# Five large blocks and 30 slots of on-chip memory, the tail's tiles ordered anew, and a 32-column product at 128 columns

## The chip, the core and the metric

The kernel runs on one core of one Trainium2 chip. The metric is device time in microseconds, the median of several runs. One more run was recorded by the hardware profiler; the profile and all queries of the trace come from it.

## The reference, cut to what matters

The input x has 16 batches of 256 tokens with 512 channels, all fp32. The first layer is a transformer block with 16 heads of 32: self-attention, cross-attention on a context, and a GELU MLP of 2048. The second layer is a recurrent block with 32 heads of 16:

```python
xxx = xa + sx * maa_x                       # xa: layer norm, sx: shifted minus xa
t = tanh(xxx @ maa_w1).reshape(B, L, 5, 32) # a product with 160 columns
m = einsum('blfd,fdc->blfc', t, maa_w2)     # five mixes w, k, v, r, g
xw, xk, xv, xr, xg = (xa + sx * (maa_j + m_j) for j in "wkvrg")
w = exp(-exp(time_decay + tanh(xw @ decay_w1) @ decay_w2))
r, k, v, g = xr @ Wr.T, xk @ Wk.T, xv @ Wv.T, silu(xg @ Wg.T)
# per head, token by token: out = r (u k v^T + s);  s = k v^T + w s
x = x + groupnorm(out) * g @ Wo.T
x = x + sigmoid(xr2 @ fWr.T) * (square(relu(xk2 @ fWk.T)) @ fWv.T)
```

## The kernel before

**Phases.** The program is written as a list of operations in phases. A is self-attention and B cross-attention, each over all 16 batches. Then come two parts of eight batches each: C0 is the MLP of batches 0 to 7, D0 the mix of the same batches (the products w, k, v, r, g), then C1 and D1 for batches 8 to 15. I0 and I1 are the "intra" work of the recurrence within groups of 8 tokens (elementwise products and sums on VectorE and GpSimd); I0 runs beside C1, I1 beside the tail. E is the tail for all 16 batches: states across the groups, reads of the states, group norm, output projection, and the last channel mix. Between phases, values go through DRAM (x1, x2, x3, and s_k, s_v, s_w, s_r, s_g, s_rp, s_ks, s_y, s_tot).

**Order.** `Sched.run` turns the list into a fixed order for each engine. It keeps a model of time, and at each step takes the operation that can start first; among equals the one with the lower index, moved by the table PRIO. DMAs all go through the one SyncE queue (L461), and their issue waits there in order. An operation can be taken only when its tiles have a place.

**Places.** `Memory` holds `SLOTS` = 34 slots of 1024 fp32 per partition (4 KB) and `BLOCKS` = 4 blocks of 4096 fp32 (16 KB), together 200 KB per partition, and the 8 banks of PSUM. A tile of class "4" takes a slot, one of class "2" half a slot (halves of one slot have one data type), one of class "16" a whole block, one of class "b" a quarter of a block. The weight tiles "wb" are of class "b". `SIZES` gives each phase a quota per tag. Earlier phases reserve what they still need: a later phase gets a place only from what the earlier ones, intra included, have neither taken nor reserved (`why_not`). So the next phase's loads and weight splits start in what is left over.

**Weights.** In A, B, C and D a weight is split into a high and a low part (`weight`, L534 and L535 with a scale, L551 and L472 without). A staging tile "st" is loaded, split on ScalarE, VectorE or GpSimd, and freed when the products for a folded bias (L522, L529) have also read it. A, B and D use 16 quarters, C uses 16 quarters and 16 slots.

**Cross-attention.** B holds up to 4 tiles of x, 3 of xh (normalised x, and the context) and 5 of xT (transposed and split; a batch needs 4). `tr` transposes (L593) and splits them (L467, L603), `attention_proj` uses them, two groups ahead of the scores.

**The mix.** `tmix` makes the 160 columns: 128 with W1, and 32 with W1b (12 products of 128 x 32 weights per batch). Tanh, and a split into `th`, high and low, follow. The parts go to a DRAM relay `tdr` and come back with other partitions, as S5 for the first four mixes and S5b for the fifth (high, low, and two rows of ones). `blend` multiplies them with W2 (L1045).

**The tail.** `tail_weights` loads eight quarters of weights (Wo, fr, fk, fv); `tail_tiles` makes the shift columns `sh0`, the constants of the channel mix, and clears two blocks VO and four slots RP (L1257), into which only the non-zero parts are written later. For each batch `states` loads VO from s_v in 8 pieces of 32 KB per half batch, multiplies (L1359), scans (L1366), reorders (L1367) and stores to `sdr`; `starts` loads it back and spreads it (L1291); `reads` transposes (L1397) and copies into RP (L1408); `heads` multiplies (L1426) and normalises; `output`, `residual` (L1471), `channels` and `finish` (L1471, L1512) do the rest. Once per four batches `states` calls `totals`, which loads s_tot, reorders (L1301), transposes (L1315) and copies it, and loads the start states s0. The intra's pieces are taken in between by `side`; I1 loads its tiles only after the gate of the last batch is stored to s_g.

Of the kernel before, what the change touches and what calls it, by code (L numbers as in the profile page):

```python
# [391 lines left out]
class Kern:  # L392
# [27 lines left out]
    def tile(self, tag, shape, name, dt=F32):  # L420
        n = 4 * int(np.prod(shape[1:]))
        h = H(tag, shape, dt, name)
        if n >= 512 or tag.startswith("p_"):
            h.phase, h.cls = self.nphase, "p" if tag.startswith("p_") else "16" if n > 4096 else tag[1] if tag in ("wb", "we") else "4" if n > 2048 else "2"
            self.mem.quota[h.phase, tag, h.cls] = self.sizes[tag]
        else:
            v = self.small.setdefault((tag, name, n), [0, []])
            if len(v[1]) < self.sizes[tag]:
                v[1].append(self.ktile(shape, name, dt))
            h = v[1][v[0] % self.sizes[tag]]  # L430
            v[0] += 1
# [466 lines left out]
class Rec(Kern):  # L898
# [7 lines left out]
    def mix_consts(self):  # L906
        I = self.I
# [3 lines left out]
        self.sh1 = self.shift_cols(1)  # L911

    def mix_weights(self):

        nc, I, tile = self.nc, self.I, self.tile
        W1, W1b, dw1 = tile("W1", [128, 4, 2, 128], "W1", F32R), tile("W1b", [128, 4, 2, 32], "W1b", F32R), tile("dw1", [128, 4, 2, 128], "dw1", F32R)
        for src, n, ws in ((I["L1_xattn_maa_w1"], 160, ((W1, 0, 128), (W1b, 128, 32))), (I["c_dw1"], 128, ((dw1, 0, 128),))):
            st = tile("st", [128, 4, n], "st")
            self.dma(st, lambda st=st: st(), lambda src=src: src.rearrange("(k p) n -> p k n", p=128), 2048 * n)
            for w, o, m in ws:  # L920
                self.split(4 * m, lambda st=st, o=o, m=m: st[:, :, o : o + m], lambda w=w: w[:, :, 0, :], lambda w=w: w[:, :, 1, :], [st], (w, 0), (w, 1))
# [20 lines left out]
        self.tdr, self.t2l = [], []  # L942
# [3 lines left out]
        for i in range(2):  # L946
            h = self.relay("tdr", [66, 5, 256], "tdr")
            self.dma(None, lambda h=h: h[64:66], lambda: fv(o2[64:66]).unsqueeze(1).to_broadcast([2, 5, 256]), 10240, r=[o2], w=[(h, 3)])
# [3 lines left out]
            self.t2l.append(h)  # L952

# [46 lines left out]
    def mix(self, src, rsrc, out, W, bs=range(B), side=None):  # L1000
# [15 lines left out]
        def tmix(b):  # L1016
# [4 lines left out]
            self.mm3((pt, 1), lambda: pt[0:32, 1, :], [lambda k=k: (W1b[:, k, 0, :], W1b[:, k, 1, :]) for k in range(4)], xs, 256, [W1b] + xx)  # L1021
            T, th = tile("T", [128, 2, 256], "tt"), tile("xj", [128, 2, 2, 256], "th", F32R)
            dr, S5, S5b = self.tdr[b % 2], tile("S5", [98, 4, 256], "S5", F32R), tile("S5b", [98, 256], "S5b", F32R)
            for i, p in ((0, 128), (1, 32)):
                emit("ACT", c_act(256), lambda i=i, p=p: nc.scalar.activation(out=T[0:p, i, :], in_=pt[0:p, i, :], func=AF.Tanh), [(pt, i)], [(T, i)])
                self.split(256, lambda i=i, p=p: T[0:p, i, :], lambda i=i, p=p: th[0:p, i, 1, :], lambda i=i, p=p: th[0:p, i, 0, :], [(T, i)], (th, (i, 1)), (th, (i, 0)))
            for x in range(2):
                self.dma(None, lambda x=x: dr[32 * x : 32 * x + 32, 0:4, :].rearrange("d j n -> j d n"), lambda x=x: fv(th[:, 0, x, :]), 131072, [(th, (0, x))], [(dr, x)])
            self.dma(None, lambda: dr[0:64, 4, :].rearrange("(x d) n -> d x n", x=2), lambda: fv(th[0:32, 1, :, :]), 65536, [(th, (1, 0)), (th, (1, 1))], [(dr, 2)])
            self.dma(None, lambda: fv(S5[0:32]), lambda: dr[32:64, 0:4, :], 131072, [(dr, 1)], [(S5, 0)])  # L1030
            self.dma(None, lambda: fv(S5[32:98]), lambda: dr[0:66, 0:4, :], 66 * 4096, [(dr, 0), (dr, 1), (dr, 3)], [(S5, 1)])
            self.dma(None, lambda: fv(S5b[0:32]), lambda: dr[32:64, 4, :], 32768, [(dr, 2)], [(S5b, 0)])
            self.dma(None, lambda: fv(S5b[32:98]), lambda: dr[0:66, 4, :], 66 * 1024, [(dr, 2), (dr, 3)], [(S5b, 1)])
# [200 lines left out]
class Tail(Rec):  # L1234
# [3 lines left out]
    def tail_weights(self):  # L1238
# [3 lines left out]
        W = {}  # L1242
        for n in ("Wo", "fr", "fk", "fv"):
            W[n] = [self.tile("wb", [128, 2, 512], "w_" + n) for _ in range(2)]
            for h, w in enumerate(W[n]):
                self.dma(w, lambda w=w: w(), lambda n=n, h=h: I["c_" + n][256 * h : 256 * h + 256, :].rearrange("(k p) c -> p k c", p=128), 524288)
        return W

    def tail_tiles(self):
        nc, I = self.nc, self.I  # L1250
        self.sh0 = self.shift_cols(0)
# [3 lines left out]
        self.RP, self.nrp = [self.tile("RP", [128, 2, 4, 4, 32], "RP") for _ in range(self.sizes["RP"])], 0  # L1255
        for t, n in [(t, 4) for t in self.VO] + [(t, 1) for t in self.RP]:
            self.emit(("POOL", "DVE"), (1250 * n, c_dve(1024 * n)), tuple(lambda t=t, e=e: e.memset(t(), 0.0) for e in (nc.gpsimd, nc.vector)), w=[t])  # L1257
# [45 lines left out]
    def totals(self, g):  # L1303

        nc = self.nc
        h = self.hin["tot"][0]
        t = self.tile("st", [128, 512], "tot")
# [9 lines left out]
        self.emit("PE", 432, fn, [t2, self.ident], [ps])  # L1317
        T = self.tile("tot", [128, 4, 4, 32], "tot")
# [9 lines left out]
        self.emit("DVE", c_dve(256), lambda: nc.vector.scalar_tensor_tensor(out=s0(), in0=m().unsqueeze(2).to_broadcast([128, 16, 16]), scalar=-1.0 / 16, in1=s0(), op0=ALU.mult, op1=ALU.add), [s0, m], [s0])  # L1328
        return T, s0

    def states(self, b):
        nc, tile, emit = self.nc, self.tile, self.emit
        if b % 4 == 0:
            self.tt = self.totals(b // 4)
# [201 lines left out]
SLOTS, BLOCKS = 34, 4  # L1536
SIZES = {
    "A": dict(wb=16, row=2, cf=1, sm=4, st=4, x=3, xh=1, xT=3, qk=3, V=3, T=6, E=9, PT=6, cT=5, mask=2, p_p=2, p_s=4, p_t=2, p_c=1),
    "B": dict(wb=16, row=2, cf=1, sm=4, st=4, x=4, xh=3, xT=5, qk=3, V=2, T=6, E=8, PT=6, cT=5, mask=4, p_p=2, p_s=4, p_t=2, p_c=1),
    "C": dict(wb=16, w=16, row=2, cf=1, sm=4, st=8, x=2, xh=2, xT=2, E=4, PT=1, cT=1, p_p=2, p_s=3, p_t=3),  # L1540
    "D": dict(wb=16, row=2, sm=4, st=4, x=1, xa=4, xx=2, W1=1, W1b=1, W2=5, dw1=1, dw2=2, t2l=2, T=3, xj=3, S5=2, S5b=2, s1=1, o=3, p_p=2, p_s=3, p_t=3, tdr=2),
# [106 lines left out]
```

## Time and profile before

| what | us |
|---|---|
| median of 3 runs (lowest, highest) | 3563.89 (3561.29, 3566.48) |
| the profiled execution | 3571.95 |
| its span | 3570.2 |
| PE (TensorE matmul) busy | 3273.7 |
| PEld (weight load, beside PE) busy | 2620.6 |
| DVE (VectorE) busy | 2843.3 |
| ACT (ScalarE) busy | 1882.5 |
| POOL (GpSimd) busy | 1395.8 |

Stages by PE's work in the trace: A to 718, B 734 to 1420, C0 1462 to 1800, D0 1800 to 2124, C1 2134 to 2490, D1 2490 to 2782, E 2782 to the end. The stretches between are where one stage hands over to the next.

To read the lines: L1359 is line 1359 of the kernel. "bank" is PSUM, "slot" and "block" the two kinds of on-chip places, "k_..." a constant; the tiles' own names are not in the trace, so a load of VO reads "block<-s_v". In a line of the timeline the first column is the start, the second the duration, in us; in brackets stands the idle time before it on its engine and what ended that. "SPq" is the SyncE queue that issues DMAs.

### The profile page before, as it was taken

The page shows a single profiled execution, that of the slowest core. Times are in us where ns is not written, and L with a number is a line of the kernel's source. Part 1 is how long each engine was busy: PE and PEld are TensorE (multiplying, and loading weights), DVE is VectorE, ACT ScalarE, POOL GpSimd, SP SyncE. Part 2 cuts the span into 40 slices and gives each one's busy share as a digit, 9 for nine tenths or more (in the row PEclk, how much of TensorE's full clock was granted, in tenths as well). Part 3 has the DMA queues.
Part 4 walks back from the last instruction along what each step waited for, and adds up shares of the span by engine and source line. Part 5 has one row for each costly group of instructions (what it writes and reads, how often), then busy time and mean ns, then how long its engine had stood idle before and what let it go on. Part 6 is the DMA issues. An engine that isn't in the chain of part 4 may idle for free. (4 is left out here: it accounts for less than half of the span.)

```text
span 3570.2 us, 72760 instructions
## 1 busy us (share of the span) xinstructions
PE 3273.7 (92%) x26978; PEld 2620.6 (73%) x26978; DVE 2843.3 (80%) x6696; ACT 1882.5 (53%) x4722; POOL 1395.8 (39%) x1853
## 2 busy tenths in 40 slices
PE   6999999989999999899999989999999558878899
PEld 4777877767777777788887879998787445555555
DVE  6888898868887788766788788899878688887653
ACT  4665666656666666433354454344444565554532
POOL 3444444444444444100021129994211476764110
PEclk9999999999999999899999999999999789998999
DMA  3111000021111110300134463343444877674420
GB/s 97 37 31 35 27 25 31 21 90 46 43 43 43 43 51 25 100 25 24 42 111 134 131 203 110 112 138 107 129 144 156 245 206 205 182 217 127 133 81 24
DMA packets 325051, 336.83 MB, mean 94 GB/s; under 512 B 40978, under 2 KB 228446, under 8 KB 324698
## 3 DMA queue, kind: packets, MB, share of 16 engines
q1 hardware_dynamic: 324698, 332.18, 30.5%
q8 instruction: 214, 3.51, 0.4%
q14 instruction: 139, 1.14, 0.1%
HBM read 199.92 MB, written 132.16 MB: 93 GB/s over the span
## 5 line engine op out<-in xcount | busy, mean ns | idle before, releaser
L721 POOL TENSOR_SCALAR slot<-slot,k_rin 128x256 f32<-128x256 f32 x1024 | 482.0, 488 | 691.8 <-DVE k_rin L718 624.8
L472 POOL TENSOR_TENSOR slot<-slot,slot 128x512 f32<-128x512 f32 (+9 forms) x394 | 540.4, 1393 | 312.7 <-ACT slot L551 133.2
L715 ACT ACTIVATE slot<-slot,k_nmx 128x256 f32<-128x256 f32 x1024 | 507.9, 498 | 199.3 <-DVE k_nmx L714 168.8
L486 PE MATMUL bank<-slot,block 128*128 128x256 f32 x1792 | 510.9, 285 | 0.2 <-ACT slot L467 0.2
L487 PE MATMUL bank<-slot,block 128*128 128x256 f32 x1792 | 508.0, 284 | 0.3 <-DVE slot L603 0.3
L488 PE MATMUL bank<-slot,block 128*128 128x256 f32 x1792 | 507.9, 283 | 0.0
L467 ACT ACTIVATE slot<-bank 128x512 f32<-128x512 f32 (+2 forms) x659 | 351.5, 565 | 270.4 <-PE bank L488 142.8
L486 PE MATMUL bank<-block,slot 128*128 128x512 f32 x1152 | 468.4, 407 | 11.3 <-ACT slot L557 10.2
L488 PE MATMUL bank<-block,slot 128*128 128x512 f32 x1152 | 453.8, 394 | 9.0 <-DVE slot L558 9.0
L487 PE MATMUL bank<-block,slot 128*128 128x512 f32 x1152 | 452.5, 393 | 0.0
L714 DVE CUSTOM_DVE_ANT_0 slot<-slot,slot 128x256 f32<-128x256 f32 x998 | 390.9, 436 | 0.0
L708 DVE SCALAR_TENSOR_TENSOR slot<-bank,slot 128x512 f32<-128x512 f32 x512 | 329.9, 680 | 44.3 <-PE bank L746 21.0
L1471 PE MATMUL bank<-block,slot 128*128 128x512 f32 x768 | 354.4, 613 | 1.6 <-DVE slot L1517 1.0
L486 PEld LDWEIGHTS bank<-slot,block 128*128 128x128 f32 x1792 | 344.1, 192 | 10.3 <-ACT slot L467 2.3
L487 PEld LDWEIGHTS bank<-slot,block 128*128 128x128 f32 x1792 | 344.0, 192 | 5.3 <-DVE slot L603 0.5
L488 PEld LDWEIGHTS bank<-slot,block 128*128 128x128 f32 x1792 | 344.1, 192 | 0.0
L487 PE MATMUL bank<-slot,slot 128*128 128x256 f32 (+2 forms) x960 | 309.1, 322 | 12.4 <-DVE slot L472 9.7
L486 PE MATMUL bank<-slot,slot 128*128 128x256 f32 (+2 forms) x960 | 307.9, 321 | 10.4 <-ACT slot L551 9.3
L734 PE MATMUL bank<-k_c,slot 128*128 128x128 f32 x2048 | 287.5, 281 | 25.1 <-POOL slot L721 10.9
L488 PE MATMUL bank<-slot,slot 128*128 128x256 f32 (+2 forms) x960 | 306.1, 319 | 1.5 <-DVE slot L558 1.5
L734 PEld LDWEIGHTS bank<-k_c,slot 128*128 128x128 f32 x2048 | 232.1, 143 | 96.3 <-POOL slot L721 64.1
L1471 PEld LDWEIGHTS bank<-block,slot 128*128 128x128 f32 x768 | 146.0, 196 | 168.6 <-issue 156.5
(195 smaller groups left out, 6639.3 us busy)
## 6 DMA issues: line engine op xcount, KB each, us to landing
slot<-in SPq DMA_DIRECT2D x153, 256.0 KB
slot<-x SPq DMA_DIRECT2D x64, 512.0 KB
x<-slot SPq DMA_DIRECT2D x48, 512.0 KB
slot<-in SPq DMA_DIRECT2D x32, 512.0 KB
sdr<-slot SPq DMA_DIRECT2D x128, 128.0 KB
slot<-sdr SPq DMA_DIRECT2D x32, 512.0 KB
s_k<-slot SPq DMA_DIRECT2D x16, 512.0 KB
s_w<-slot SPq DMA_DIRECT2D x16, 512.0 KB
```

What stands on the lines that cost most here:

```text
L467: self.emit(("ACT", "DVE"), (c_act(n), c_dve(n)), (lambda: nc.scalar.activation(out=out(), in_=in_(), func=AF.Copy), lambda: nc.vector.ten ...
L472: self.emit(("DVE", "POOL"), (c_dve(n), c_pool(n)), (lambda: nc.vector.tensor_tensor(out=out(), in0=in0(), in1=in1(), op=op), lambda: nc.g ...
L486: nc.tensor.matmul(o, lhsT=lh, rhs=rh, start=first and i == 0, stop=False)
L487: nc.tensor.matmul(o, lhsT=lh, rhs=rl, start=False, stop=False)
L488: nc.tensor.matmul(o, lhsT=ll, rhs=rh, start=False, stop=last and i == k - 1)
L708: emit("DVE", c_dve(512), lambda j=j, T=T: nc.vector.scalar_tensor_tensor(out=T(), in0=ps[j](), scalar=-scale, in1=mask(), op0=ALU.mult, o ...
L714: emit("DVE", c_dve(256) + 80, lambda T=T, j=j, qt=qt: nc.vector.tensor_tensor_reduce(out=T[:, qt, :], in0=T[:, qt, :], in1=negb[:, qt, :] ...
L715: emit("ACT", c_act(256, 1, 1), lambda T=T, Et=Et, j=j, qt=qt: nc.scalar.activation(out=Et[:, qt, :], in_=T[:, qt, :], func=AF.Exp, scale= ...
L721: emit("POOL", 470, lambda jj=jj, qt=qt: nc.gpsimd.tensor_scalar(out=E[jj][:, qt, :], in0=E[jj][:, qt, :], scalar1=rin[:, qt, jj : jj + 1] ...
L734: nc.tensor.transpose(pt[:, k, 128 * qt : 128 * qt + 128], E[j][:, qt, 128 * k : 128 * k + 128], self.ident())
L1471: self.nc.tensor.matmul(po(), lhsT=x[k // 2][:, k % 2, ts], rhs=w[k // 2][:, k % 2, :], start=k == 0, stop=k == 3)
```

## The change

Its core:

```diff
-            ... else tag[1] if tag in ("wb", "we") else ...
+            ... else tag[1] if tag in ("wb", "we", "rb") else ...
-SLOTS, BLOCKS = 34, 4
+SLOTS, BLOCKS = 30, 5
 SIZES = {
-    "B": dict(... x=4, xh=3, xT=5, ...
+    "B": dict(... x=3, xh=2, xT=4, ...
-    "C": dict(wb=16, w=16, ...
+    "C": dict(wb=20, w=12, ...
-    "D": dict(... s1=1, ...
+    "D": dict(... s1=2, ...
-    "E": dict(... RP=4, ...
+    "E": dict(... rb=4, ...
```

The total stays 200 KB per partition. C has 20 weights in blocks and 12 in slots. RP goes from slots into quarters of a block.

```diff
# mix_consts
-        self.sh1 = self.shift_cols(1)
+        self.sh1, self.sh0 = self.shift_cols(1), self.shift_cols(0)
# mix_weights: W1b [128, 4, 2, 32] becomes [128, 4, 2, 128], its 32 columns four times over
+                rows = lambda w, x, m=m: w[:, :, x, :].rearrange("p k (r c) -> p k r c", c=m)
+                self.split(512, lambda st=st, o=o, m=m: st[:, :, o : o + m].unsqueeze(2).to_broadcast([128, 4, 128 // m, m]), ...)
-            h = self.relay("tdr", [66, 5, 256], "tdr")
+            h = self.relay("tdr", [66, 4, 256], "tdr")
+            h = tile("S5b", [98, 256], f"S5b{i}", F32R)
# tmix
-            self.mm3((pt, 1), lambda: pt[0:32, 1, :], ...
+            self.mm3((pt, 1), lambda: pt[:, 1, :], ...
-            T, th = tile("T", [128, 2, 256], "tt"), tile("xj", [128, 2, 2, 256], "th", F32R)
+            T, th = tile("T", [128, 2, 256], "tt"), tile("s1", [128, 2, 256], "th", F32R)
-            for i, p in ((0, 128), (1, 32)):
+            for i, p in ((0, 128), (1, 96)):
                 emit("ACT", c_act(256), ... activation(out=T[0:p, i, :], in_=pt[0:p, i, :], func=AF.Tanh) ...
-                self.split(256, ... th[0:p, i, 1, :] ... th[0:p, i, 0, :] ...
+            self.split(256, lambda: T[:, 0, :], lambda: th[:, 1, :], lambda: th[:, 0, :], [(T, 0)], (th, 1), (th, 0))
-            self.dma(None, lambda: dr[0:64, 4, :]..., lambda: fv(th[0:32, 1, :, :]), 65536, ...)
-            self.dma(None, lambda: fv(S5b[0:32]), lambda: dr[32:64, 4, :], 32768, ...)
-            self.dma(None, lambda: fv(S5b[32:98]), lambda: dr[0:66, 4, :], 66 * 1024, ...)
+            emit(("ACT", "DVE"), ..., copy S5b[0:96] <- T[0:96, 1, :], [(T, 1)], [(S5b, 0), (S5b, 1)])
+            self.sub(256, lambda: S5b[32:64], lambda: T[32:64, 1, :], lambda: fv(S5b[32:64]), [(T, 1), (S5b, 0)], [(S5b, 1)])
```

Two S5b are kept for the whole phase, their rows 96 and 97 set to one at its start. The 32 columns come out four times, on all 128 partitions of PSUM, so that high, low and high part of the fifth mix are made where they are needed, without the way through DRAM.

```diff
+    def tail_consts(self):            # the column constants, taken out of tail_weights
     def tail_weights(self):
-                self.dma(w, ..., 524288)
+                self.dma(w, ..., 524288, [self.turn])
     def tail_tiles(self):
-        self.sh0 = self.shift_cols(0)
-        self.RP, self.nrp = [self.tile("RP", ...
+        self.RP, self.nrp = [self.tile("rb", ...
+        self.turn = H(None, None, None, "turn")
         for t, n in [(t, 4) for t in self.VO] + [(t, 1) for t in self.RP]:
-            self.emit(("POOL", "DVE"), ..., memset ..., w=[t])
+            self.emit(("POOL", "DVE"), ..., memset ..., [self.turn], [t, self.turn] if n > 1 else [t])
     def totals(self, g, within=None):
+        last = self.phase(within) if within else None
...
+        if last:
+            self.phase("E")
         T = self.tile("tot", [128, 4, 4, 32], "tot")
...
+        if last:
+            self.phase(last)
     def states(self, b):
-            self.tt = self.totals(b // 4)
+            self.tt = self.totals(b // 4) if b else self.first
# block_kernel
-        k.mix(rows(x3), lambda b: [(h3, b)], to, W, bs)
+        begun = []
+        def first_totals():
+            begun.append(1)
+            if n and len(begun) == 20:
+                k.hin = at
+                k.first = k.totals(0, k.now)
+        k.mix(rows(x3), lambda b: [(h3, b)], to, W, bs, first_totals)
     k.phase("E")
+    k.tail_consts()
+    k.tail_tiles()
     W = k.tail_weights()
-    k.tail_tiles()
```

`turn` is a handle without memory: each VO clear reads and writes it, RP's clears and the weights' loads read it. So the two VO clears come first, one behind the other, and RP and the weights behind both. The first totals are written into the list after the 20th of the second mix's 40 steps, with the PSUM bank and staging tiles of that phase, and with their result and the start states in tiles of E.

## Prediction

> **What bounds the kernel now.** I read the page's busy shares and slices first, then a table of busy time by stage, then PE's waits at each place where a stage hands over to the next. The page:
>
> ```profile
> span 3570.2 us, 72760 instructions
> PE 3273.7 (92%) x26978; PEld 2620.6 (73%) x26978; DVE 2843.3 (80%) x6696; ACT 1882.5 (53%) x4722; POOL 1395.8 (39%) x1853
> ```
>
> PE is busy 3273.7 of 3570.2 us. The change takes no product off PE, so what it can win lies in the 296.5 us in which PE idles. Stage by stage (columns: length; PE, PEld, DVE, ACT, POOL busy; granted clock; DMA share; GB/s):
>
> ```profile
> 718.00:734.00 16.00, 7.80 (x27) 4.23 (x26) 9.13 (x22) 7.58 (x12) 5.67 (x4) 0.88 0.85 287
> 734.00:1420.00 686.00, 660.35 (x5537) 536.72 (x5540) 555.36 (x1821) 446.27 (x1378) 288.30 (x543) 0.99 0.13 40
> 1420.00:1462.00 42.00, 24.32 (x230) 15.33 (x223) 32.14 (x69) 24.98 (x55) 15.35 (x19) 0.76 0.59 187
> ...
> 2124.00:2134.00 10.00, 0.40 (x4) 0.20 (x2) 8.19 (x15) 7.71 (x15) 3.79 (x3) 0.62 1.03 318
> ...
> 2782.00:2850.00 68.00, 28.59 (x924) 25.65 (x923) 41.21 (x77) 38.96 (x90) 33.06 (x32) 0.70 0.77 223
> 2850.00:3250.00 400.00, 322.48 (x4272) 205.47 (x4271) 353.60 (x608) 235.06 (x507) 280.21 (x244) 0.89 0.69 198
> 3250.00:3570.00 320.00, 290.58 (x2627) 175.42 (x2624) 181.60 (x404) 130.64 (x275) 42.71 (x78) 0.96 0.28 85
> ```
>
> The idle of PE is length minus its busy time: 8.2 us where attention A hands over to B, 17.7 from B to the first MLP, 9.6 from the first mix to the second MLP, 39.4 in the tail's first 68 us. From 2850 to 3250 VectorE is at 353.6/400 = 88% and carries the second intra beside the tail; from 3250 PE is at 91% and works off what has piled up. So a tail that starts earlier leaves a smaller pile, and the end comes earlier. The opening, in PE's order of time, and all that PE waits for in the tail:
>
> ```profile
> 2771.22 3.47 DVE L1257 MEMSET block<- 128x4096 f32 x1 [0.93 <-PE bank L488]
> 2775.86 3.52 POOL L1257 MEMSET block<- 128x4096 f32 x1 [20.89 <-PE bank L488]
> ```
>
> ```profile
> 2781.76 1.91 PE L1397 MATMUL bank<-k_c,slot 128*128 128x128 f32 x16
> 2786.07 1.90 PE L1359 MATMUL bank<-block,slot 128*32 128x128 f32 x64 [2.40 <-DMA block<-s_v]
> 2797.26 3.16 PE L1359 MATMUL bank<-block,slot 128*32 128x128 f32 x55 [9.29 <-DMA block<-s_v]
> ...
> 2802.72 3.27 PE L1359 MATMUL bank<-block,slot 128*32 128x128 f32 x64 [1.93 <-DMA block<-s_v]
> ...
> 2819.11 3.16 PE L1359 MATMUL bank<-block,slot 128*32 128x128 f32 x56 [13.11 <-DMA block<-s_v]
> ```
>
> ```profile
> PE bank L1359 <- DMA block<-s_v: 48.4, 8, 13.1
> ```
>
> Both VO blocks are cleared only at 2771 and 2776, when the second mix gives up the blocks of its weights; the tail's weights take the block before them (first issue at 2770). Four halves of the first two batches wait 2.4 + 9.3 + 1.9 + 13.1 = 26.7 us for VO's loads, of 48.4 in the whole tail. These loads share the DMA engines with 8 x 512 KB of tail weights.
>
> **The change, part by part.**
>
> *The tail's opening.* With five blocks the second mix uses four (16 weight quarters), so the first VO can be cleared and filled with batch 0 inside the mix, and the second takes the first block that is freed (the k weights' last product ends near 2763) instead of the third; the weights come behind both. The first half's product can then run before 2782, the second by 2782 instead of 2797: 15 us earlier. Batch 1 follows a refill later: its second half comes at about 2803 for 2819, 16 us. What cannot follow is the intra (its loads are issued at 2801 behind the last gate store, as now) and VectorE: it idles 68.0 - 41.2 = 26.8 us here, of which only that before the 88% stretch, in 2785 to 2830, can be filled, about 18. Bounds: no gain (VectorE's later work swallows it) to 18; below nothing by 5, since RP's four clears now wait for the VO clears (they ran at 2695 to 2729 now, POOL L1257, 0.95 us each; the first use is the copy at 2782). I take 12, near the upper rows, because two thirds of this idle is PE waiting for a load that the change moves.
>
> *Totals and shift columns.* The first totals are one 256 KB load, one copy (0.62), 4 transposes, one copy (0.68), all done by 2777 now, ahead of 2786. Moved, they gain nothing by themselves: 0. The wait they add: their PSUM bank, one of the mix's two p_p, is held until an E slot is free. Units of half slots: the mix keeps 52 of 60, the intra 15, so none is free for E before the mix winds down. The mix's other p_p users (front, tmix, decay) then queue for one bank for up to two batches of 36 us. Price 0 to 6; I take 1.
>
> *Fifth block at the other hand-overs.* A to B: the query weights can be split during A. Now the second half of their split is at 710.6 to 713.3, and the loads of the next weights are issued from 709; their staging tiles could be free when the bias products end, at 700. What then ends last is the load of the context:
>
> ```profile
> 710.61 2.73 DVE L535 SCALAR_TENSOR_TENSOR block<-slot,k_l2s,block 128x512 fp32r<-128x512 f32 x4
> ```
>
> ```profile
> 731.38 2.79 PE L593 MATMUL bank<-k_c,slot 128*128 128x128 f32 x12 [4.64 <-DMA slot<-in]
> ```
>
> One megabyte less in this stretch is 1.05 MB/287 GB/s = 3.7 us; at most all 8.2. I take 4, from -2 (fewer slots for B's early loads: A keeps 53 half slots, so 7 of 60 are free for them instead of 15 of 68). B to the first MLP: PE waits 17.3 us for staged weights, the longest one:
>
> ```profile
> 1457.47 0.66 PE L522 MATMUL bank<-slot,k_l3b 128*32 128x128 f32 x8 [10.02 <-DMA slot<-in]
> ```
>
> The same reasoning; B keeps 56 of 60 half slots, so 4 are free for staging instead of 6, so I take 4 of -3 to 10. First mix to second MLP: the 9.8 us wait is for the first GELU and the next weights; each pair gets its block one projection earlier (some 6 us), but staging slots are fewer: 2 of 0 to 6. First MLP to mix: PE is at 334.98/338, nothing to win.
>
> *Fewer x, xh and xT in B.* The fifth xT tile could be used ahead of the last projection. It isn't: the last projection's products end at 1023.9 and the four transposes follow at 1026.0, 1028.4, 1030.3 and 1031.9, the next projection at 1033.2, with scores, mixes and transposes of weights between. The cover is 9.3 us of other products per batch. Cost 0 to 2 per batch; I take 2 us in all for 15 batches.
>
> *Small product at full width.* 12 products per batch get a 128-column weight. Its loads, one narrow, one wide, in the first mix:
>
> ```profile
> L488 PEld LDWEIGHTS bank<-slot,slot 128*128 128x128 f32 x72 | 15.5, 215 | 0.9 <-DVE slot L558 0.4
> L488 PEld LDWEIGHTS bank<-slot,slot 128*32 128x32 f32 x28 | 3.8, 134 | 0.7
> ```
>
> That is +81 ns for each of 192 loads, 15.6 us if bare. But products of both widths start 0.12 us apart at full clock (narrow at 1915.06, 1915.18, 1915.29; wide at 1940.56, 1940.68, 1940.80), so the load lies beside the product before it: 0. In return three DMAs per batch (64, 32 and 66 KB) and their SP issues (3 x about 0.6 us) go, and the fifth tanh row set no longer passes DRAM; it is needed only four steps later, so 0. The splits into a four times wider W1b add about 0.5 us twice, at hand-overs: inside the range.
>
> The Trainium skill, "TensorE: Matmul & The Clock Gate", section "LDWEIGHTS (loading the stationary operand)", speaks against this edit: a load's time is its columns over 1.2 per ns, so 32 to 128 columns is 27 to 107 ns. By that rule 192 x 80 ns = 15.4 us would be added if nothing hid it, and the gain below would shrink to about 5 us. The row has a smaller ratio (134 to 215) and shows the start-to-start distance unchanged.
>
> **Sum.** Gains 12 + 4 + 4 + 2 = 22, costs 1 + 2 = 3, so 19 us, rounded to 20. The profiled execution took 3571.95 us (span 3570.2 and 1.75 around it): 3552. It lies 8.1 above the median of the three runs, 3563.89, so on their scale I forecast **3544**.
>
> **Rivals.**
> 1. *The opening is won and lost again.* If VectorE at 88% from 2850 to 3250 and the intra, whose start does not move, set the pace, the 12 us go and 4 + 4 + 2 - 3 = 7 remain: 3557. For: VectorE's and POOL's steps make up most of the chain of waits in this stretch. Against: PE idles 77.5 us there, and the last 320 us are PE's.
> 2. *Only the opening gains.* Staging slots, not blocks, limit the hand-overs; 12 - 3 = 9: 3555.
> 3. *Slower: the channel tiles of B.* With four xT tiles for four needed, all transposes must lie between the last projection of a batch and the first of the next. If the new order leaves this 6.6 us chain (1026.0 to 1032.6) partly bare, 2.5 us in each of 15 batches is 37 us: 3544 + 37 = 3581. It turns the sign from 20/15 = 1.3 us per batch, and is outside 0.2% from 1.8. For: no spare tile is left, and VectorE, which must split all four, is at 555/686 = 81%. Against: 9.3 us of cover.
> 4. *It doesn't do what it says.* The first VO gets no block early, because the mix's reservations or a block left partly filled keep it out: opening 0, hand-overs little: 3562.
>
> **How the numbers follow.** Chances: forecast 0.42, rivals one 0.13, two 0.12, three 0.25, four 0.08. A difference under 0.2% (7 us) is about what a measurement of this kernel can't tell from no change. Faster: the forecast, two, and most of one: 0.42 + 0.12 + 0.09 = 0.63; same: the rest of one and four: 0.12; slower: three: 0.25. Range: the best bounds (18 + 8 + 10 + 6, nothing lost) are 42 us, 3522, and the order being new throughout, 3518; the other end takes in rival three: 3582. The forecast's own range is 3525 to 3554.
>
> **What would show it.** Right: one VO clear during the second mix, the other near 2763 on today's clock, L1359's waits for s_v down from 48.4 by 20 or more, the four first halves 12 to 16 us earlier relative to the mix's last product; L535 into blocks before A's last group; narrow 128*32 loads gone with D's stage length unchanged at 324 and 292 us. Wrong: B longer than 686 us with waits at L593, or a second mix longer than 292 (bank held), or an opening that is shorter while 3250 to the end is no shorter.

## The result and the profile after

After takes **3591.54 us** (median of 4 runs, 3590.38 to 3596.53), before 3563.14 on the same chip: ratio **1.0077, 95% interval 1.0063 to 1.0092**. It is 28 us slower; 3544 was forecast, and the range ended at 3582. The profiled execution of after is 3590.38 us long, span 3588.6.

The page of after:

```profile
span 3588.6 us, 72653 instructions
PE 3289.7 (92%) x26978; PEld 2628.6 (73%) x26978; DVE 2875.0 (80%) x6693; ACT 1874.5 (52%) x4716; POOL 1415.7 (39%) x1866
```

PE's products are the same in number. VectorE executes 3 instructions fewer and is busy 31.7 us longer (2875.0 for 2843.3): the prediction has no term for this.

Stage by stage, read from the times at which SP issues the stores (first and last store of x1, x2, x3, the gate and the output), in the two profiled executions. The times were rounded before they were subtracted, so a row can be off by 1 us:

| from store to store | before | after |
|---|---|---|
| A's end to B's first | 78 | 64 |
| B | 653 | 650 |
| B's end to C0's first, C0 (7 batches) | 66, 283 | 64, 278 |
| to D0's first gate, D0 | 69, 250 | 79, 252 |
| to C1's first, C1 | 62, 325 | 58, **341** |
| to D1's first gate, D1 | 32, 251 | **38**, 251 |
| last gate to last output (the tail) | 778 | **790** |

Of C0 only seven batches are counted, since its eighth store comes behind D0's first gate.

These rows add up to +18 us; the rest of the 28 is that before's profiled execution lay 8 above its median and after's 1 below. So A to B, B, B to C0, C0 and D0 to C1 gave 14 + 3 + 2 + 5 + 4 us. The hand-over into the first mix, C1 beside the intra, the hand-over into the second mix, and the tail took 10 + 16 + 6 + 12, with 2 in D0.

The three windows of after that answer to those shown of before (hand-over A to B, and the tail's stretches, laid from 6 us later):

```profile
718.00:734.00 16.00, 14.55 (x97) 11.03 (x96) 10.06 (x19) 6.72 (x12) 6.89 (x4) 1.00 0.53 185
...
2856.00:3256.00 400.00, 311.81 (x4120) 195.85 (x4118) 353.56 (x554) 231.28 (x502) 262.21 (x226) 0.89 0.63 187
3256.00:3588.00 332.00, 306.55 (x2676) 183.66 (x2676) 197.91 (x426) 138.13 (x294) 67.71 (x102) 0.96 0.29 92
```

A to B, PE idles 1.5 us for 8.2. In the 400 us of the tail VectorE is as busy as before (353.6 us), but does 554 instructions for 608, and PE 311.8 us for 322.5: VectorE's instructions take longer on the mean.

The opening, VO's clears first, then PE's products on VO (timelines of after):

```profile
2476.29 3.52 POOL L1264 MEMSET block<- 128x4096 f32 x1
2767.37 3.52 POOL L1264 MEMSET block<- 128x4096 f32 x1 [6.05 <-PE bank L488]
```

```profile
2758.82 1.05 PE L1371 MATMUL bank<-block,slot 128*32 128x128 f32 x32
2760.24 1.05 PE L1371 MATMUL bank<-block,slot 128*32 128x128 f32 x32
...
2795.80 5.20 PE L1371 MATMUL bank<-block,slot 128*32 128x128 f32 x128 [7.95 <-DMA block<-s_v]
2813.11 3.39 PE L1371 MATMUL bank<-block,slot 128*32 128x128 f32 x64 [11.08 <-DMA block<-s_v]
```

```profile
PE bank L1371 <- DMA block<-s_v: 31.0, 4, 11.1
```

The first half product comes at 2759 for 2786, inside the mix. Against the last gate store (2789 before, 2795 after) the four halves are 33, 7, 10 and 12 us earlier, and the waits for s_v fall from 48.4 to 31.0. Still the first output comes only 4 us earlier against that store (178 us behind it for 182), and the last one 12 us later.

### The profile page after: what moved, and what is told of

Read it like the earlier page. It is cut to its first block, busy times and chain, and to the rows that moved or that the text cites. A ratio compares the mean times of both kernels' runs of the same rounds, so it can differ in the third digit from the quotient of the medians.

```text
span 3588.6 us, 72653 instructions
## 1 busy us (share of the span) xinstructions
PE 3289.7 (92%) x26978; PEld 2628.6 (73%) x26978; DVE 2875.0 (80%) x6693; ACT 1874.5 (52%) x4716; POOL 1415.7 (39%) x1866
## 5 line engine op out<-in xcount | busy, mean ns | idle before, releaser
L487 PE MATMUL bank<-slot,block 128*128 128x256 f32 x2048 | 581.9, 284 | 6.7 <-DVE slot L558 4.2
L486 PE MATMUL bank<-slot,block 128*128 128x256 f32 x2048 | 584.5, 285 | 0.8 <-ACT slot L467 0.5
L488 PE MATMUL bank<-slot,block 128*128 128x256 f32 x2048 | 581.5, 284 | 0.0
L487 PEld LDWEIGHTS bank<-slot,block 128*128 128x128 f32 x2048 | 394.1, 192 | 13.3 <-DVE slot L558 4.6
L486 PEld LDWEIGHTS bank<-slot,block 128*128 128x128 f32 x2048 | 394.0, 192 | 12.1 <-ACT slot L467 2.9
L488 PEld LDWEIGHTS bank<-slot,block 128*128 128x128 f32 x2048 | 394.0, 192 | 0.0
L1483 PEld LDWEIGHTS bank<-block,slot 128*128 128x128 f32 x768 | 149.4, 201 | 189.0 <-issue 166.6
L486 PEld LDWEIGHTS bank<-block,slot 128*128 128x128 f32 x1152 | 218.4, 190 | 65.2 <-issue 14.6
L488 PEld LDWEIGHTS bank<-block,slot 128*128 128x128 f32 x1152 | 217.4, 189 | 62.2 <-DVE slot L558 14.9
L486 PE MATMUL bank<-slot,slot 128*128 128x256 f32 (+1 forms) x704 | 237.5, 337 | 22.2 <-ACT slot L557 9.3
```

The lines of the kernel that those rows point to most:

```text
L486: nc.tensor.matmul(o, lhsT=lh, rhs=rh, start=first and i == 0, stop=False)
L487: nc.tensor.matmul(o, lhsT=lh, rhs=rl, start=False, stop=False)
L488: nc.tensor.matmul(o, lhsT=ll, rhs=rh, start=False, stop=last and i == k - 1)
L1483: self.nc.tensor.matmul(po(), lhsT=x[k // 2][:, k % 2, ts], rhs=w[k // 2][:, k % 2, :], start=k == 0, stop=k == 3)
```

## Where VectorE's time went

The groups that grew are the smallest instructions of the tail. `heads` makes the group norm's reciprocal root on VectorE in twelve steps of 64 elements per batch; here three of the steps, before and after (mean ns of one behind the comma):

```profile
L1442 DVE SCALAR_TENSOR_TENSOR k_gr<-k_gt,k_gr 128x64 f32<-128x64 f32 x48 | 15.2, 316 | 1.6
L1441 DVE TENSOR_TENSOR k_gt<-k_gt,k_gr 128x64 f32<-128x64 f32 x48 | 14.4, 299 | 1.6
L1440 DVE SCALAR_TENSOR_TENSOR k_gt<-k_gr,k_gv 128x64 f32<-128x64 f32 x48 | 13.3, 278 | 1.6
```

```profile
L1453 DVE TENSOR_TENSOR k_gt<-k_gt,k_gr 128x64 f32<-128x64 f32 x48 | 25.0, 521 | 1.6
L1452 DVE SCALAR_TENSOR_TENSOR k_gt<-k_gr,k_gv 128x64 f32<-128x64 f32 x48 | 21.5, 447 | 1.4
L1454 DVE SCALAR_TENSOR_TENSOR k_gr<-k_gt,k_gr 128x64 f32<-128x64 f32 x48 | 20.5, 426 | 1.6
```

All 192 steps take 64.9 us in before and 89.7 in after (the groups' means give 64.5 and 89.4); 192 times the shortest duration of each form is 40, so 25.0 and **50.0 us** are excess. The cause stands in the timelines of VectorE and GpSimd in after, side by side:

```profile
3016.06 0.30 DVE L1452 SCALAR_TENSOR_TENSOR k_gt<-k_gr,k_gv 128x64 f32<-128x64 f32 x1
3016.40 1.20 DVE L1453 TENSOR_TENSOR k_gt<-k_gt,k_gr 128x64 f32<-128x64 f32 x1
3017.64 1.19 DVE L1454 SCALAR_TENSOR_TENSOR k_gr<-k_gt,k_gr 128x64 f32<-128x64 f32 x1
...
3023.33 2.26 DVE L1453 TENSOR_TENSOR k_gt<-k_gt,k_gr 128x64 f32<-128x64 f32 x1
3025.62 2.26 DVE L1454 SCALAR_TENSOR_TENSOR k_gr<-k_gt,k_gr 128x64 f32<-128x64 f32 x1
```

```profile
3016.25 1.28 POOL L472 TENSOR_TENSOR slot<-slot 128x512 f32<-128x512 f32 x1
3017.48 5.05 POOL L472 TENSOR_TENSOR slot<-slot,slot 128x512 f32<-128x512 f32 x4
3022.49 0.72 POOL L472 TENSOR_TENSOR slot<-slot 128x256 f32<-128x256 f32 x1
3023.17 8.19 POOL L472 TENSOR_TENSOR slot<-slot,slot 128x1024 f32<-128x1024 f32 x4
```

The step at 3016.40 ends at 3017.60, 0.07 us behind the end of the product that GpSimd began at 3016.25 (3017.53). From there each step lasts as long as one product of the intra: 1.2 us beside products of 512 elements, 2.26 beside 1024, for 0.21 alone. It is so throughout: all 47 steps of after that take over 0.5 us, and all 23 of before, end 0.05 to 0.09 us behind the end of a GpSimd instruction, and none of those of up to 0.3 us lies inside one. In the model of time that makes the order, such instructions of the two engines never overlap (`port` in `Sched.run`); in the rows they do. The waits table shows none of it, since the wait lies inside the instruction: it is found by comparing a group's mean with its shortest.

The Trainium skill, "SBUF — State Buffer", section "SBUF: two separate sides", has the rule: VectorE (in some modes, or with two operands from SBUF) and GpSimd share a port pair, and whoever starts first keeps it for the whole instruction. The rows agree, at 2.3 us at the longest.

## Experiments

Chips differ (before took 3563 to 3572 us), so ratios are to before on the same chip. The bracket is the excess of the 192 small steps.

| | ratio (95%) | C1 | to D1 | tail | small steps, us |
|---|---|---|---|---|---|
| before | 1 | 325 | 32 | 778 | 64.9 (25.0) |
| after | 1.0077 (1.0063-1.0092) | 341 | 38 | 790 | 89.7 (50.0) |
| e1 after, steps as sums | 0.9978 (0.9969-0.9988) | 340 | 39 | 761 | 42.0 |
| e2 before, steps as sums | 0.9985 (0.9976-0.9995) | 328 | 32 | 771 | 42.1 |
| e3 memory alone | 1.0057 (1.0041-1.0073) | 337 | 39 | 796 | 65.0 (24.6) |
| e4 all but memory | 1.0014 (1.0005-1.0024) | 330 | 31 | 792 | 54.1 (13.3) |
| e5 after, bias on ScalarE | 1.0047 (1.0031-1.0064) | 334 | 38 | 792 | 90.7 (51.2) |
| e6 after, root in PSUM | 0.9962 (0.9947-0.9977) | 343 | 38 | 751 | 43 |
| e7 before, root in PSUM | 0.9992 (0.9981-1.0003) | 325 | 32 | 769 | 43 |
| e8 after, e5 and e6 | **0.9929 (0.9915-0.9944)** | 334 | 38 | 746 | 43 |
| e9 no early totals | 1.0045 (1.0029-1.0061) | 341 | 39 | 779 | 71.7 (31.7) |
| e10 no tail order | 1.0061 (1.0039-1.0082) | 344 | 41 | 781 | 73.7 (34.0) |
| e11 no wide product | 1.0005 (0.9993-1.0017) | 337 | 43 | 774 | 67.6 (27.6) |
| e12 memory and tail order | 1.0015 (1.0005-1.0025) | 337 | 43 | 779 | 72.3 (32.5) |
| e13 tail's blocks later | 1.0081 (1.0057-1.0104) | 340 | 42 | 786 | 95.5 (56.4) |
| e14 e8 and e13 | 0.9954 (0.9937-0.9971) | 334 | 37 | 754 | 43 |
| e15 normalise first | 1.0114 (1.0099-1.0129) | 342 | 40 | 790 | 88.0 (48.5) |
| e16 before, e5 and e6 | 1.0097 (1.0081-1.0112) | 340 | 35 | 795 | 43 |
| e17 normalise as sums | 1.0037 (1.0023-1.0051) | 334 | 38 | 788 | 89.0 (49.6) |
| e18 e8, normalise on ScalarE | 0.9946 (0.9929-0.9962) | 337 | 44 | 748 | 43 |

### The small steps, in the same order (e1, e2)

Each of the twelve steps becomes a sum over an axis of length one; the order stays, instruction by instruction:

```diff
-  nc.vector.tensor_tensor(out=t(), in0=t(), in1=r(), op=ALU.mult)
+  nc.vector.tensor_reduce(out=t(), in_=t().unsqueeze(2), axis=AX.X, op=ALU.add)
```

> The kernel after, in its own order, but the twelve small steps of 64 elements per batch with which the group norm makes its reciprocal root (L1446 to L1454) are replaced by sums over an axis of length one: same tiles, same sizes, same place in the order. The reciprocal root is left out by this, so the output is not the reference's. In the trace of after these 192 steps take 89.7 us, 50.0 more than 192 times their shortest durations, and each long one ends about 0.1 us behind the end of a GpSimd product; before they take 64.9, 25.0 more than their shortest. Sums (L1445) show no such lengthening. Port theory (the new order lays these steps beside GpSimd's products, VectorE paces the tail at 88%, and this is what the tail loses): the steps take about 45 us, VectorE loses some 45 us in the tail, and the time falls by 25 to 45 us, to 3547 to 3567. Rival (the steps are off the path, PE waits for other things): within 6 us of after, 3586 to 3598.

> The same replacement in the kernel before, again with its own order kept and the reciprocal root left out. Port theory: here only 25.0 us can go, so the time falls by 10 to 25 us, to 3538 to 3553, and the distance from after to before, 28 us, shrinks to 15 or less. Rival: within 6 us of before, 3557 to 3569, and the distance of 28 us stays.

The steps of e1, in the same places beside the same products:

```profile
L1454 DVE TENSOR_REDUCE k_gr<-k_gt 128x64 f32<-128x64 f32 x48 | 10.6, 220 | 1.6
L1453 DVE TENSOR_REDUCE k_gt<-k_gt 128x64 f32<-128x64 f32 x48 | 10.5, 220 | 1.6
```

No excess is left. After's time falls by 1.0077 - 0.9978 = 1.0%, some 35 us, and its tail by 29 us; before's by 0.15% (5 us; 10 to 25 were expected, a miss), its tail by 7. The two are then within 0.1% of each other: **the waits cost after 22 us more of tail than before**. In the 400 us from 2856 VectorE is then busy 332 us for 354, and PE 326 for 312 (e1's row):

```profile
2856.00:3256.00 400.00, 326.45 (x4306) 205.40 (x4304) 332.41 (x588) 244.60 (x540) 284.98 (x244) 0.90 0.67 195
```

Without the waits after's first output comes 14 us earlier behind the last gate store than before's (166, 181) and the last one 10 us earlier (761, 771). That fits a gain of the opening of the size forecast; it isn't shown to be the opening's alone, since the rest of the tail's order differs too.

### The small steps with one operand in PSUM (e6, e7)

One operand of each step lies in the PSUM bank that has just been read; the reference is computed in full:

```diff
-  r = tile("gs", [128, 64], "gr")
+  r = lambda: py().rearrange("p e a v -> p (e a v)")[:, 64:128]   # v, t stay in SBUF
```

> The kernel after, with one operand of each of the twelve small steps in PSUM, in the bank from which the last group's sum has just been read, so that no step has all its operands in SBUF; the whole reference is computed. The products L1429 (before) and L1441 (after), with one operand in PSUM, always take 0.68 us beside GpSimd. Port theory: no step over 0.5 us, 192 steps in 45 to 55 us against 89.7, the length from the last gate store to the end 760 to 772 for 790, and a total of 0.9965 to 1.0005 of before. Rival (the steps wait for GpSimd whatever they read, or the bank held some 4 us longer per batch stops PE): steps above 70 us or PE waits at L1438 for banks, and a tail of 780 or more.

> The same edit of the twelve steps in the kernel before. Port theory, with e2 as its size: 192 steps in 45 to 55 us against 64.9, the tail 768 to 776 for 778, total 0.997 to 1.000 of before; so that after with the edit (e6) ends within 0.2% of before with it, or below. Rival: tail 780 or more.

In e6:

```profile
L1454 DVE SCALAR_TENSOR_TENSOR k_gt<-bank,k_gv 128x64 f32<-128x64 f32 x48 | 10.7, 223 | 1.6
L1455 DVE TENSOR_TENSOR k_gt<-k_gt,bank 128x64 f32<-128x64 f32 x48 | 10.6, 220 | 1.6
```

No step takes over 0.23 us; the tail takes 751 us (760 to 772 expected) and the total is 0.9962, both better than the ranges given. The order behind these steps is a new one here, so the 10 us between e1 and e6 are not the steps'. Before gains 0.08%, not told from nothing, and its tail 9 us. With this hazard out of both, after is 0.3% (11 us) faster than before (e6, e7).

### The parts (e3, e4, e9 to e12)

Each kernel takes parts of the diff: the memory (SLOTS, BLOCKS, the sizes of B and C, RP in quarters), the tail's order (`turn`, tiles ahead of weights), the totals in the mix, and the wide product. For e3, for example:

```diff
-SLOTS, BLOCKS = 34, 4
+SLOTS, BLOCKS = 30, 5
```

> The kernel before with the memory part alone: five blocks and 30 slots, the sizes of B and C that go with them, RP in quarters of a block; the tail's order, the totals and the narrow product stay as before. If the memory part makes both the gains at the hand-overs and the losses: first store of B 14 us earlier than before, last store of the first layer's second half (C1) level with before, as after shows, and a total above before by 10 to 30 us. If the losses come from the tail's order, the totals or the wide product: the hand-over gains stay to the end, 3563 less some 15, 3540 to 3555. Port theory: whatever the part, the length from the last gate store to the end moves with the excess of the small steps, some 0.5 us per us.

> The kernel after without the memory part: four blocks and 34 slots and the sizes of before, RP in slots; the tail's order, the totals in the second mix and the wide product stay as in after. If the memory part makes the losses: no gain at the hand-over of A to B, C1 as before, total within 8 us of before, 3555 to 3571. If the other three parts make them: C1 or the tail longer by 15 to 30 us and a total of 3578 to 3600, above after's since the hand-over's 14 us are missing. Port theory: length of the tail against the excess of the small steps as in the other runs.

> The kernel after without the early totals: the first totals are made at the first states again, the rest as in after. So far the small steps wait for GpSimd 25.0 us in before, 50.0 in after, 24.6 with the memory alone, 13.3 with all but the memory. Theory of chance (no single part lays the steps beside GpSimd's products; every new order deals the meetings anew, between some 10 and 50 us): the excess is anywhere in 10 to 50, and the tail's length follows it by some 0.6 us per us around 764 (after: 790 at 50). Theory of one part (the totals' move does it): excess below 25 and tail below 778, and with the next two runs near 50.

> The kernel after without the tail's new order: weights ahead of the tail's tiles and no turn among the clears, with the memory, the totals and the wide product of after. Chance: excess of the small steps anywhere in 10 to 50. One part (the tail's order lays them there): excess 25 or less. Beside that, the opening: the half products of VO wait for s_v some 20 us longer and the first stores of the intra or of the output come 8 to 16 us later relative to the last gate than in after (178 us from there to the first output), as the prediction has it; if the opening is worth nothing, they come within 4 us.

> The kernel after without the wide product: 32 columns, the fifth mix through DRAM again. Prediction: the second mix's length (251 us from first to last gate store) within 3 us of after's, the cost of the wide loads being hidden. If the loads are not hidden: 6 to 8 us shorter than after's per mix. Chance: excess of the small steps anywhere in 10 to 50; one part (the wide product): 25 or less.

> The kernel before with the memory part and the tail's order alone; totals and product as before. Second MLP as in after and e3, 336 to 342 us. The opening's gain needs these two parts only: the distance from the last gate store to the first output is 170 to 180 (before 182, memory alone 189, after 178). Chance: excess anywhere in 10 to 50, total between 0.998 and 1.007 of before, 0.6 us per us of excess. If totals or wide product do harm of their own, total below 1.002 with an excess like after's.

No one part lays the steps beside the products: without the totals, the tail's order or the wide product the excess falls from 50 to 28 to 34 us, and without the memory part to 13. With all four parts it is no matter of luck from run to run: after, e5, e13, e15 and e17 have 48 to 56. Where memory and tail order are in, the tail goes with the excess: 761 us at 2 (e1), 774 at 28, 779 at 32, 790 at 50, or 0.6 us per us (e13, 786 at 56, lies below). It is no law: with no excess, e6, e8, e14 and e18 have tails of 746 to 754, and e3 and e4 lie above that line. In e4 VO is cleared only at 2769 and 2774, since no block is free for it before, and RP and the weights wait behind it: PE does 31 us of work in the opening's 85 us, for 46 of 86 in before. In e3 PE waits 17.7 us once for the spread start states (L1426).

The memory part alone makes the gain from A to B (64 us in e3, 77 in e4), 6 of the 9 to 10 us more into D0 (75 in e3, 71 in e4, 79 in after), the longer way into D1 (39 for 32), and most of C1 (337 for 325). The way into D0 also takes 76 us in e16, with four blocks and another order, so five blocks aren't needed for that.

With the tail's order left out (e10), the first store of s_y by the intra comes 15 us later against the last gate (102 for 87 us) and the first output 6 (184 for 178). But PE's waits for s_v are shorter there, 20.4 us for 31.0, where 20 more were expected. And s_y is as late in e9 (104) and e12 (106), which have the tail's order without the early totals, while before has 86 without either. So what the tail's order is worth by itself is not shown. The totals' held bank costs nothing that shows (D1 takes 246 to 252 us in the kernels without it, 243 to 253 in those with it). Without the wide product D0 and D1 take 253 and 245 us for 252 and 251, between the two ranges expected; D1 is as short in e10 and e13 (246, 245), which have it, so no cost of it shows.

### The second MLP (e5, e13, e15, e17)

```diff
# e5: L852
-  emit(("ACT", "DVE"), (c_act(256, 1), c_dve(256, 1)), (lambda ...activation, lambda ...tensor_scalar), ...)
+  emit("ACT", c_act(256, 1), lambda ...activation, ...)
# e13: the clears in tail_tiles
-  [self.turn], ...
+  [self.turn, (self.hin["g"][0], 8)], ...
# e15: PRIO
-  "C.lnst": 100, "C.lnrs": 400
+  "C.lnst": -400, "C.lnrs": -400
# e17: L575, L577, L580 on VectorE in C
+  nc.vector.tensor_reduce(out=xh[:, t, :], in_=x[:, t, :].unsqueeze(2), ...)
```

> The kernel after, with the MLP's bias adds (L852) given to ScalarE alone, as one of the two engines that could take them; nothing else is changed, and the order is made anew from there. From the first to the last store of x3 in the second MLP after takes 341 us, before 325, and memory alone (e3) 337; PE's waits there are for VectorE (L580, L558, L603), which has 58 bias adds of 0.49 us in after, 57 in e3 and 43 before, while ScalarE idles 60%. Theory (VectorE paces the second MLP, and the new places pushed bias adds onto it): 28 us of VectorE's work go from this stage, its length falls to 323 to 332 and the hand-over to the second mix from 38 to 32 to 36; the total falls by 8 to 20 us if the tail's small steps wait as in after (50 us), and more if fewer of them do. Rival (loads or splits are late since there are fewer free slots): the stage stays at 338 to 344.

> The kernel after, but both VO clears (and so RP's and the tail's weights behind them) also wait for the first gate of the second mix to be stored. In after the fifth block comes free at the end of the second MLP, and the tail takes it at once: 8 loads of s_v stand in SP's queue at 2481 to 2496, between the loads of the second mix's weights. Theory (the tail's early block disturbs the hand-over): from the last store of x3 to the first gate 32 to 34 us instead of 38, and PE's wait of 5.2 us at L486 before 2510 shorter; the opening of the tail (178 us to the first output) stays within 4 us, since 250 us of the mix are left to fill the block. Total 4 to 8 us below after, if the small steps still wait some 50 us. Rival (the hand-over is late because the second MLP's last GELU is): 37 to 40 us as before, and the total within 4 us of after's.

> The kernel after with the statistics of the MLP's layer norm taken first among equals (two priorities of the order changed, from 100 and 400 to -400). In after PE waits 6.0 us in the second MLP for the normalised x (L580), each gap of 1 to 2.4 us, and one such gap comes with a granted clock of 0.91 for its 20 us. Theory (the normalise chain, behind GpSimd's products, is what lengthens the second MLP): waits at L593 under 2 us and 332 to 337 us from first to last x3 for 341. Rival (VectorE as a whole is late there, whichever step is taken first): the waits move to L558 and L603, and the stage stays at 338 to 344.

> The kernel after, in its own order, but in the two MLP stages VectorE's three steps of the layer norm (L575, L577, and L580 where VectorE has it) are replaced by sums over an axis of length one, of the same size and place, that still wait for GpSimd's power step (L576). The normalisation is left out by this, so the output is not the reference's. In after, in front of PE's gaps of 1.30 and 1.08 us at 2333 to 2335, L577 takes 1.24 us and two L580 2.98 us (0.2 and 0.5 each elsewhere), between products of GpSimd. Port theory for the second MLP: no such step is lengthened, PE's waits at L593 go from 6.0 us below 3, and with them the granted clock's dips; the stage goes from 341 to 333 to 337 us, the total falls by 4 to 10 us. Rival (the order lays statistics, GpSimd's power step and the normalise too late in any case): the waits stay at 4 us or more and the stage at 338 to 344.

In e5 C1 is 7 us shorter, 334, outside both ranges (323 to 332, 338 to 344). Its order is new there, the bias adds between these stores are 47 in after and 37 before, and VectorE is busy only 3 us more in C1 of after than of before (299 for 296), so that VectorE's load is a part of the 16 us is not shown. In e13 the hand-over takes 42 us, longer than either side expected: the tail's loads in SP's queue are not what delays it. In e15 C1 stays at 342, as the rival had it, but the waits didn't move away from L593; they rose to 9.5 us. So taking the statistics first doesn't help.

Lengthened steps show here too. PE's waits in C1 for the normalised x (L593) and for the splits (L557, L558), before and after:

```profile
PE bank L593 <- DVE slot L580: 1.8, 3, 1.0
...
PE bank L488 <- DVE slot L558: 1.5, 3, 0.6
PE bank L486 <- DVE slot L557: 1.0, 1, 1.0
```

```profile
PE bank L593 <- DVE slot L580: 6.0, 5, 1.7
PE bank L488 <- DVE slot L558: 4.8, 6, 1.5
PE bank L486 <- ACT slot L557: 3.7, 2, 2.5
```

One wait for the normalised x in after, VectorE, then PE:

```profile
2330.62 1.24 DVE L577 SCALAR_TENSOR_TENSOR k_lnnb<-k_lnmv,k_lnrs 128x2 f32<-128x2 f32 x1
2331.89 2.98 DVE L580 TENSOR_SCALAR slot<-slot,k_lnrs,k_lnnb 128x512 f32<-128x512 f32 x2
```

```profile
2333.52 0.33 PE L593 MATMUL bank<-k_c,slot 128*128 128x128 f32 x1 [1.30 <-DVE slot L580]
2334.92 1.76 PE L593 MATMUL bank<-k_c,slot 128*128 128x128 f32 x7 [1.08 <-DVE slot L580]
```

The same two places in e17 (its lines lie 1 to 3 further down), in the same order:

```profile
2330.74 0.16 DVE L578 TENSOR_REDUCE k_lnnb<-k_lnrs 128x2 f32<-128x2 f32 x1
2330.82 1.27 DVE L583 TENSOR_REDUCE slot<-slot 128x512 f32<-128x512 f32 x2
```

L577's place takes 0.16 us for 1.24, L580's 1.27 for 2.98. PE's waits at the transposes fall from 6.0 to 1.2, C1 from 341 to 334, the total by 0.4% (14 us). So **7 us of C1 in after hang on the same kind of wait**. That they are 7 of the 16 us between before and after is not shown: the excess of these three steps in C1 is 7.3 us in before and 8.8 in after, hardly more, only that in after more of it lies in front of PE (waits of 6.0 us for 1.8), and the same edit in before was not run. PE's waits for the splits (L557, L558) went from 2.5 us to 8.5, and e17 leaves them as they are (9.1).

### Both together (e8, e14, e16, e18)

e8 has the edits of e5 and e6, e14 that of e13 too, e16 those of e8 in before. In e18, on top of e8:

```diff
-  nc.vector.scalar_tensor_tensor(out=nb(), in0=mv[:, :, 0], scalar=-1.0, in1=rs(), ...)
+  nc.gpsimd.tensor_tensor(out=nb(), in0=nm(), in1=rs(), op=ALU.mult)   # nm: minus the mean
-  self.emit(("DVE", "POOL", "ACT"), ..., fns, ...)                     # L580
+  self.emit("ACT", c_act(512, 2) + 43, fns[2], ...)
```

> The kernel after with both edits: bias adds of the MLP on ScalarE alone, and one operand of the small steps in PSUM. If both theories hold: second MLP 323 to 332, tail 760 to 772, total 0.992 to 0.997 of before, faster than both kernels. If only the port theory holds: second MLP 338 to 344 and a total of 0.997 to 1.000. If neither: above 1.003.

> Kernel e8 (bias adds on ScalarE, small steps with an operand in PSUM) with the tail's blocks later as in e13. Theory: hand-over 32 to 34 for 38, tail 745 to 755 as in e8, total 0.990 to 0.993 of before. Rival: hand-over 37 to 40, total 0.992 to 0.995.

> The kernel before with the two edits of e8: bias adds on ScalarE alone, small steps with an operand in PSUM. It completes the square before/after by without/with. If the change itself is a gain once VectorE's two hazards are out: e16 lies 0.2 to 0.6% above e8, at 0.995 to 0.999 of before; second MLP 322 to 326, hand-over of A to B 78, tail 765 to 772. If after's hand-overs give back what they win: e16 within 0.2% of e8, 0.991 to 0.995.

> Kernel e8 with the layer norms of the MLP and the tail taken off VectorE: the product of mean and reciprocal root on GpSimd behind its power step, the normalise on ScalarE alone; the whole reference is computed, and the order is made anew. Port theory: waits at L593 in the second MLP below 3 us, the stage 326 to 333 us (e8 334), tail 738 to 750 (e8 746), total 0.988 to 0.993 of before. Rival (each new order deals the second MLP anew, 330 to 344 in the runs so far, and the port is only one of its cards): stage 334 to 344, total 0.993 to 1.000.

e8 is faster than both kernels, by 25 us against before. e16 is the warning: the same two edits in before make it 1% slower. C1 takes 340 us there and not 325, PE waits 10.2 us at L580, and the tail takes 795 us without one long small step. VectorE is busy 556 us of that tail, 549 in e7, so these 26 us are not VectorE's; their cause is open. C1 takes 325 to 328 only in before, e2 and e7, which keep its order up to there, and 330 to 344 in every order made anew, with four blocks or five. So at least 9 of C1's 16 us go with the new order as such; which step of it is not settled. e14's hand-over takes 37 us, as its rival had it, and its total is 0.2% above e8's, so the later blocks gain nothing here either. e18's rival held: PE waits 0.8 us in C1 for the normalised x, and C1 still takes 337.

## Why the prediction was wrong, step by step

- **The step that failed**: that the gain of the opening goes through to the end, "near the upper rows, because two thirds of this idle is PE waiting for a load that the change moves". The load did move (33, 7, 10 and 12 us earlier for 12 to 16 forecast), and with the small steps out of the way the tail is 10 us shorter than before's, for 12 (e1, e2). But VectorE, at 88%, paces the next 400 us, and the new order gave it 25 us more, so the tail came out 12 us longer: durations of the one profile were carried over to an order in which other instructions run beside them. Rival 1 had the mechanism (VectorE swallows the gain) and too small a price, since it let VectorE's work stay the same. Its own sign of being wrong came up: an opening that is shorter while the last stretch, 320 us before, is 332.
- **The whole distance.** On the profile's scale 3552 was forecast and 3590 came. Of these 38 us the tail is 24 (12 gained in the forecast, 12 lost), C1 16, the ways into the two mixes 16 and D0 2; the other hand-overs, B and C0 gave 28 where 7 were forecast, 21 less. Only rival 3 foresaw a slower kernel, and for a reason that the runs don't show.
- **C1** was not priced at all: +16. Up to 7 of them are waits behind lengthened steps (e17, without its counterpart in before), and at least 9 come with the order (open).
- **Hand-overs.** A to B 14 us for 4, above the bound of 8.2. The mechanism held: the query weights' split (L534, L535), at 691 to 713 in before, is done by 46 us in after. From 680 to the first store of x2 PE's idle time falls from 15.3 to 7.0 us, and the mean granted clock there is 0.98 for 0.91, which fits the rest (PE's busy time falls from 103.1 to 96.7 us, with 778 and 764 products). B to the first MLP 2 and 5 inside it for 4; first mix to second MLP 4 for 2. "First MLP to mix ... nothing to win" forgot that something can be lost: +10, and +6 into the second mix. With the memory part alone they are +6 and +7 (e3).
- **Right in size**: the held bank (1; nothing shows), the channel tiles of B (2; B is 3 us shorter in after and 1 longer in e3, so rival 3 falls), the wide product (0; no cost shows).
- The gains forecast, 22 us, came and more: 28 at the hand-overs, in B and in C0, and, with the waits out, a tail 10 us shorter. The part of A to B's 14 us beyond the bound was luck: the clock was in no term of the sum. What was missing is a term for the new order in the stages where VectorE and GpSimd work side by side.

## What to carry to other kernels

A change that moves memory makes a new order, and a new order changes durations: where VectorE and GpSimd both read SBUF, price small VectorE steps by their shortest and their longest row (0.21 and 2.3 us here), and compare a group's mean with its minimum in both profiles before looking for waits. Keep one operand of such steps in PSUM, as e6 does, which brought after from 0.8% above before to 0.4% below. A gain in an opening is worth its time only if the engine that paces the next stage has room for it.

## What the runs showed of the hardware

- A VectorE step of 64 elements with all operands in SBUF takes 0.21 us alone and up to 2.3 beside a GpSimd product; with one operand in PSUM at most 0.23, and sums of the same size 0.22, beside the same products. Steps with a single SBUF input are lengthened too (L1450 from 0.19 to 2.30, L580 from 0.5 to 1.5 us each).
- A gap of PE can come with a lower clock. In the 20 us with the gaps of 1.30 and 1.08 us in C1 of after the granted clock is 0.91, where it is 1.00 in the 20 us before and behind. It isn't always so: from 740 to 760, in A to B of after, PE idles 2.5 us and the clock is 1.00. The row of C1:

```profile
2330.00:2350.00 20.00, 17.16 (x95) 14.44 (x95) 17.93 (x21) 5.60 (x11) 16.70 (x14) 0.91 0.19 52
```
